# An output gate built from tanh, two halves for every output, and rows fetched two outputs in advance

## The chip, the cores and the metric

The program runs on one core of one Trainium2 chip. A core has five engines that each work through their own list of instructions in order: TensorE (PE) multiplies matrices, VectorE (DVE) and ScalarE (ACT) work element by element, GpSimd (POOL) here computes small statistics and issues some DMAs, and SyncE (SP) issues the other DMAs. An engine's list is fixed when the program is built. An instruction that waits holds up all that stand behind it on its engine.

The metric is the device time of one launch in microseconds. Before the change the median of 3 runs was 1276.79 us (1276.71 to 1282.77).

## The reference

The input x is 16 sequences of 512 tokens with 256 channels. It is normalized once (xn), and two branches work on xn. The first is a recurrent block with its own normalizations, a scan over time and a feed-forward part. The second is a mixture of 8 experts: each token goes to one expert, whose result is weighted by a router's probability. The two meet in a gate.

```python
    xn = _layernorm(x, axis=-1)
    s = _L0_attn_ref(xn, ...)              # recurrent branch
    g = _silu(_L0_ffn_ref(xn, Wg, W1, W2)) # experts, each token weighted by its router's probability
    x = x + s * g
```

In the experts' part the output row of a token is `weights * (gelu(xt @ W1[e]) @ W2[e])` for the expert e that holds the token. So the gate of a token's row y with weight w is silu(w·y), and the output is x + s·silu(w·y).

## The kernel before

The work is cut by sequence: `recurrent(b, done)` is the recurrent branch for sequence b, written as a Python generator in 9 steps. The list `steps` says in which order the 16 generators advance; three sequences are under way at a time. Beside it, `rest_of` advances other generators: the router, the weights' loads, 36 to 39 units of expert work (`expert`, 256 tokens each), and at the end `outputs`. A scheduler then orders the instructions on each engine within what the dependencies allow.

A sequence's tensors are four tiles of 128 tokens by 256 channels (1024 numbers in each of 128 partitions). In a sequence's branch come, in order:

- `normed`: statistics on DVE (L216, L218), one over the root on POOL (L209 and L210, the latter a power), the scale on ACT (L226);
- `shifted` and `mix`: transposes on PE (L234), ACT L515 and L522, DVE L523;
- the projections k, v and r on PE (L556), put out of PSUM by ACT (L628, L632, L636);
- `wkv` twice, once for each half of the channels: on DVE a scan L575, L579, L580, on ACT three Relus (L581 to L583) and an Exp (L584), then on DVE L585 to L594, with the reciprocal L593 of 3.35 us in it. Its result is vT;
- the product o with WoT (PE L599, added to x0 on DVE at L646), `normed` again (its POOL part computes nm and rs), `shifted` and `mix`;
- the products f (PE L556), each put out by ACT with Relu (L659) and squared (L660);
- twice, for half of the sequence each: a product fr (PE L599), its tanh on ACT (L669), a product kv (PE L599), then on DVE L673 and L675, which finish that half of x0, the recurrent branch's s.

PSUM buffers for fr, kv and o come from one pool of two. So kv of the second half can begin only when L673 of the first half has read kv of the first.

For b below `LATE` = 14, s is put into a scratch in memory by `keep`. The experts put their rows into another scratch, `ys_d`, by indirect DMAs from POOL (L722). When all experts have ended, a branch taken on the device (L744) separates the experts from the outputs. `outputs` then takes s (tag `w2` or `x`) and the experts' rows y (tag `w1`, two buffers) of sequences 0 to 13 back from memory, and `output` does four Silu on ACT (L755), with the router's weight as the scale of each tile, one product on DVE (L756), and one DMA from POOL (L757) that adds the product to what is in `out`. The input x had been copied to `out` earlier (L654). Sequences 14 and 15 are put out by `put` straight from x0. The outputs run while the branches of sequences 13, 14 and 15 end.

In the routing, `route` ends in a loop of four groups that makes one-hot tables on DVE (L464, L470, L473, L474) and multiplies them on PE (L479).

Of the kernel before, what the change touches and what calls it, by code (L numbers as in the profile page):

```python
# [9 lines left out]
F32 = mybir.dt.float32  # L10
I32 = mybir.dt.int32
F16 = mybir.dt.float16
AF = mybir.ActivationFunctionType
ALU = mybir.AluOpType
# [5 lines left out]
P = 128  # L20
# [6 lines left out]
def rwkv_times_moe_kernel(ctx: ExitStack, tc: tile.TileContext, a, out: bass.AP):  # L27
# [10 lines left out]
    nc = tc.nc  # L38
    x = a["x"]
    B, T, C = x.shape  # L40
# [3 lines left out]
    NJ = T // P  # L44
# [11 lines left out]
    work = ctx.enter_context(tc.tile_pool(name="work", bufs=1))  # L56
# [52 lines left out]
    place_of = const.tile([P, NJ], F32, name="place_of")  # L109
# [60 lines left out]
    ys_d = dram.tile([B * T + NR * R, C], F32, name="ys_d")  # L170
    s_d = dram.tile([B * T, C], F32, name="s_d")

    def tokens_of(t, b):

        return t[b].rearrange("(j p) c -> p j c", p=P)

    def rows_of(t, b):

        return t[b * T : (b + 1) * T].rearrange("(p j) c -> p (j c)", p=P)
# [3 lines left out]
    def flat(t):  # L183
        return t.rearrange("p j c -> p (j c)")
# [6 lines left out]
    weight_of = const.tile([P, NT], F32, name="weight_of")  # L191
# [7 lines left out]
    def load(src, b, name, tag="x", bufs=2):  # L199
        t = work.tile([P, NJ, C], F32, tag=tag, bufs=bufs, name=f"{name}{b}")  # L200
        if src is x:
            nc.sync.dma_start(t, tokens_of(x, b))
        else:
            nc.sync.dma_start(flat(t), rows_of(src, b))
        return t

    def inv_std(rs, var):

        nc.gpsimd.tensor_scalar(rs, var, EPS, None, ALU.add)  # L209
        nc.gpsimd.tensor_tensor(rs, rs, power, ALU.pow)  # L210
# [71 lines left out]
    def route():  # L282
# [117 lines left out]
        one = buf[0]  # L400
# [5 lines left out]
        ahead = work.tile([P, 1], F32, tag="prior", name="ahead")  # L406
# [52 lines left out]
        def spread(v, t0, n):  # L459
            return v[:, t0 : t0 + G, None].to_broadcast([P, G, n])  # L460

        for t0 in range(0, NT, G):
            in_lo = work.tile([P, G, P], F16, tag="kf", bufs=KF, name=f"in_lo{t0}")
            nc.vector.tensor_tensor(  # L464
                in_lo, spread(lo, t0, P), count_s[:, None, :].to_broadcast([P, G, P]), ALU.is_equal
            )

            in_hi = work.tile([P, G, 3, NS], F16, tag="ex", bufs=2, name=f"in_hi{t0}")
            one, place, seq = (in_hi[:, :, i, :] for i in range(3))
            nc.vector.tensor_tensor(  # L470
                one, spread(hi, t0, NS), count_s[:, None, :NS].to_broadcast([P, G, NS]), ALU.is_equal
            )
            nc.vector.tensor_scalar(place, one, place_of[:, t0 // B : t0 // B + 1], None, ALU.mult)  # L473
            nc.vector.tensor_tensor(  # L474
                seq, one, count_s[:, :B, None].to_broadcast([P, B, NS]), ALU.mult
            )
            yield
            for g in range(G):
                nc.tensor.matmul(  # L479
                    table, lhsT=in_lo[:, g, :], rhs=in_hi[:, g],  # L480
                    start=(t0 + g == 0), stop=(t0 + g == NT - 1),
                )
# [17 lines left out]
    def normed(src, name):  # L500

        mv = work.tile([P, NJ, 2], F32, tag="mv", bufs=3, name=f"mv_{name}")
        rs = work.tile([P, NJ], F32, tag="rs", bufs=3, name=f"rs_{name}")
        moments(mv, src, name)
        inv_std(rs, mv[:, :, 1])
        n = work.tile([P, NJ, C], F32, tag="tok", bufs=TOK, name=f"n_{name}")
        normalize(n, src, mv[:, :, 0], rs, name)
        return n
# [93 lines left out]
        if jj or n > NC:  # L602
            then_route(mm)

    def recurrent(b, done):

        xn = at_hand.pop(b) if b in at_hand else load(xn_d, b, "xc")

        g = slice(b * NJ, (b + 1) * NJ)
        r0 = work.tile([P, NJ], F32, tag="r0", bufs=2, name=f"r0_{b}")  # L610
        nc.gpsimd.tensor_tensor(r0, rs_all[:, g], rs_all[:, g], ALU.mult)
        nc.gpsimd.tensor_tensor(r0, r0, mv_all[:, g, 1], ALU.mult)
        inv_std(r0, r0)
        x0 = work.tile([P, NJ, C], F32, tag="x0", bufs=3, name=f"x0_{b}")
        for j in range(NJ):
            nc.vector.scalar_tensor_tensor(
                x0[:, j, :], xn[:, j, :], r0[:, j : j + 1], ln0w, ALU.mult, ALU.mult
            )
        nc.vector.tensor_tensor(x0, x0, ln0b[:, None, :].to_broadcast([P, NJ, C]), ALU.add)
        n1 = normed(x0, f"1_{b}")  # L620
        yield
        hp = shifted(n1, "ln1_w", "ln1_b", f"1_{b}")
        yield

        xk = mix(hp, "tmk", f"k{b}")
        kT = f4(f"kT{b}", "kT", 2)
        for o in range(NC):
            nc.scalar.copy(kT[:, o, :], project(wk, xk, o, f"k_{b}_{o}"))  # L628
        xv = mix(hp, "tmv", f"v{b}")
        vT = f4(f"vT{b}", "vT", 2)  # L630
        for o in range(NC):
            nc.scalar.copy(vT[:, o, :], project(wv, xv, o, f"v_{b}_{o}"))  # L632
        xr = mix(hp, "tmr", f"r{b}")
        erT = f4(f"erT{b}", "erT", 2)
        for o in range(NC):
            nc.scalar.activation(erT[:, o, :], project(wr, xr, o, f"r_{b}_{o}"), AF.Exp, scale=-1.0)  # L636
        yield
        for h in range(NC):
            wkv(kT, vT, erT, h, f"{b}_{h}")
            yield  # L640

        for j0 in range(0, NJ, 2):
            ps = pp_ot.tile([P, 2, C], F32, tag="ot", name=f"o_{b}_{j0}")
            for jj in range(2):
                token_major(lambda c, j: vT[:, c, j * P : (j + 1) * P], wo, NC, j0 + jj, ps, jj)
            nc.vector.tensor_tensor(x0[:, j0 : j0 + 2, :], x0[:, j0 : j0 + 2, :], ps, ALU.add)  # L646

        n2 = normed(x0, f"2_{b}")
        yield
        hp2 = shifted(n2, "ln2_w", "ln2_b", f"2_{b}")  # L650
        yield
        xk2 = mix(hp2, "cmk", f"k2{b}")
        xr2 = mix(hp2, "cmr", f"r2{b}")
        nc.sync.dma_start(rows_of(out_rows, b), rows_of(x_rows, b))  # L654
        kf = []
        for q in range(NH // 2):
            t = work.tile([P, 2, T], F32, tag="kf", bufs=KF, name=f"kf{b}_{q}")
            for o in range(2):
                nc.scalar.activation(t[:, o, :], project(wfk, xk2, q * 2 + o, f"f_{b}_{q}_{o}"), AF.Relu)  # L659
            nc.scalar.activation(t, t, AF.Square)  # L660
            kf.append(t)
        yield
        for j0 in range(0, NJ, 2):
            psr = pp_ot.tile([P, 2, C], F32, tag="ot", name=f"fr_{b}_{j0}")
            for jj in range(2):
                token_major(lambda c, j: xr2[:, c, j * P : (j + 1) * P], wfr, NC, j0 + jj, psr, jj)

            fr = work.tile([P, 2, C], F32, tag="fr", bufs=2, name=f"frs_{b}_{j0}")
            nc.scalar.activation(fr, psr, AF.Tanh, scale=0.5)  # L669
            psv = pp_ot.tile([P, 2, C], F32, tag="ot", name=f"kv_{b}_{j0}")  # L670
            for jj in range(2):
                token_major(lambda c, j: kf[c // 2][:, c % 2, j * P : (j + 1) * P], wfv, NH, j0 + jj, psv, jj)
            nc.vector.scalar_tensor_tensor(fr, fr, 1.0, psv, ALU.add, ALU.mult)  # L673
            xo = x0[:, j0 : j0 + 2, :]
            nc.vector.scalar_tensor_tensor(xo, fr, 0.5, xo, ALU.mult, ALU.add)  # L675
        done(b, x0)
        yield

    DEEP = 3
# [66 lines left out]
                pass  # L746


    def fetch(b):
        return (load(ys_d, b, "y", tag="w1"),)  # L750

    def output(b, s, y):
        for j in range(NJ):
            t = j * B + b
            nc.scalar.activation(y[:, j, :], y[:, j, :], AF.Silu, scale=weight_of[:, t : t + 1])  # L755
        nc.vector.tensor_tensor(s, s, y, ALU.mult)  # L756
        nc.gpsimd.dma_start(tokens_of(out, b), s, accum_op=ALU.add)  # L757

    def keep(b, x0):
        nc.sync.dma_start(rows_of(s_d, b), flat(x0))  # L760

    def put(b, x0):
        output(b, x0, *fetch(b))

    def outputs(bs):

        ahead = None
        for b in bs:

            now = b, load(s_d, b, "s", tag="w2" if b < 6 or b % 2 else "x"), *fetch(b)  # L770
            if ahead:
                output(*ahead)
            ahead = now
            yield
        output(*ahead)
        yield


    def each(f, items):
# [4 lines left out]

    STEPS, LATE = 9, 14
    branch = [recurrent(b, keep if b < LATE else put) for b in range(B)]
    steps = [0, 0, 0, 1, 0, 1, 0]
    for b in range(B):  # L790
        steps += [i for i in (b, b + 1, b, b, b + 1, b + 2, b, b + 1, b + 2) if i < B]
# [73 lines left out]
```

## Time and profile before

| what | us |
|---|---|
| median of 3 runs | 1276.79 |
| the profiled execution's own time | 1279.82 |
| its span, from the first to the last instruction | 1278.0 |
| mean granted clock of TensorE | 0.956 |
| PE busy in the span | 1132.0 |
| PEld (weight load) busy | 776.2 |
| DVE busy | 762.2 |
| ACT busy | 734.8 |
| POOL busy | 331.9 |

The 1.8 us between the execution's own time and its span lie outside the first and the last instruction. Times in the trace are microseconds from the span's start. The last expert's rows are written near 1098, the branch is passed near 1099, and what follows up to 1278 is called the tail here: the end of sequences 13, 14 and 15 of the recurrent branch, with all 16 outputs beside it. In rows of a group, the first number after the bar is the group's busy time, the second the mean time of one instruction in nanoseconds, and behind the second bar stands the idle time of the engine before these instructions and what ended it.

### The profile page before, as it was taken

The numbers are of one execution on the slowest core, as the hardware profiler recorded it, in microseconds if no ns is written. First come the engines' busy times: TensorE is split into PE (matmuls) and PEld (weight loads), VectorE is DVE, ScalarE is ACT, GpSimd is POOL, SyncE is SP. The second block draws the span as 40 slices with busy tenths as digits, with TensorE's granted clock in tenths as the row PEclk, the third lists the DMA queues.
The fourth block names the chain that finished last, engine by engine and source line by source line (L and its number), as shares of the span: only waits on it lengthen the run. The fifth ranks groups of instructions, "written<-read, shape, count | busy, mean of one in ns | idle before, by whom it ended". The sixth has DMA issues, their size and how long they took to land. (4 is left out here: it accounts for less than half of the span.)

```text
span 1278.0 us, 12598 instructions
## 1 busy us (share of the span) xinstructions
PE 1132.0 (89%) x4333; PEld 776.2 (61%) x4333; DVE 762.2 (60%) x1245; ACT 734.8 (57%) x1190; POOL 331.9 (26%) x427
## 2 busy tenths in 40 slices
PE   4888979579999899999999999999999989795966
PEld 2444736346668486665867667586766848463634
DVE  6887767994473727547272654727366472566651
ACT  4775774245482736638383673838356272684951
POOL 6512020051332223233241323314232210213020
PEclk9997989888999999999999999999999999898978
DMA  7761020331233122222231232223222311279391
GB/s 238 236 251 49 11 89 1 115 107 58 83 107 107 50 99 94 87 84 74 96 99 62 83 99 83 74 94 101 62 82 88 100 35 47 96 176 211 74 193 18
DMA packets 67116, 125.11 MB, mean 98 GB/s; under 512 B 5846, under 2 KB 43244, under 8 KB 66796
## 3 DMA queue, kind: packets, MB, share of 16 engines
q1 hardware_dynamic: 51692, 97.02, 22.9%
q0 software_dynamic: 15360, 27.27, 9.3%
q8 instruction: 35, 0.57, 0.2%
q14 instruction: 29, 0.24, 0.1%
HBM read 90.72 MB, written 41.94 MB: 104 GB/s over the span
## 5 line engine op out<-in xcount | busy, mean ns | idle before, releaser
L556 PE MATMUL f<-mix_k,WfkT_sb 128*128 128x512 f32 x512 | 241.2, 627 | 28.2 <-DVE mix_k L523 18.7
L599 PE MATMUL kv<-WfvT_sb,kf 128*128 128x256 f32 x1024 | 229.4, 380 | 0.0
L599 PEld LDWEIGHTS kv<-WfvT_sb,kf 128*128 128x128 f32 x1024 | 193.5, 190 | 25.7
L722 POOL DMA_INDIRECT ys_d<-ys,goes x72 | 80.0, 1111 | 494.9 <-ACT ys L720 332.9
L556 PEld LDWEIGHTS f<-mix_k,WfkT_sb 128*128 128x128 f32 x512 | 99.6, 200 | 152.7 <-issue 104.7
L673 DVE SCALAR_TENSOR_TENSOR frs<-frs,kv 128x512 f32<-128x512 f32 x32 | 21.9, 683 | 243.2 <-PE kv L599 243.1
L599 PE MATMUL y<-w,act 128*128 128x256 f32 x576 | 132.3, 380 | 2.3 <-ACT act L713 1.9
L708 PE MATMUL h<-xsT,w 128*128 128x256 f32 x576 | 130.2, 379 | 0.0
L599 PEld LDWEIGHTS y<-w,act 128*128 128x128 f32 x576 | 107.9, 190 | 23.5 <-issue 6.8
L708 PEld LDWEIGHTS h<-xsT,w 128*128 128x128 f32 x576 | 109.4, 190 | 17.0 <-issue 2.2
L691 POOL DMA_INDIRECT xs<-xn_d,holds x72 | 78.6, 1091 | 131.8 <-DVE of L489 73.1
L226 ACT ACTIVATE n<-x,nm,rs 128x256 f32<-128x256 f32 x128 | 68.5, 593 | 76.6 <-POOL nm L224 76.5
L593 DVE RECIPROCAL ex<-ex 128x512 f32<-128x512 f32 x32 | 107.2, 3351 | 0.8
L659 ACT ACTIVATE kf<-f 128x512 f32<-128x512 f32 x128 | 74.1, 593 | 47.3 <-PE f L556 46.6
L669 ACT ACTIVATE frs<-fr 128x512 f32<-128x512 f32 x32 | 19.0, 594 | 117.5 <-PE fr L599 117.4
L585 DVE TENSOR_TENSOR_SCAN ba<-ex 128x512 f32<-128x512 f32 x32 | 38.8, 1213 | 70.9 <-ACT ex L584 70.8
L556 PE MATMUL r<-mix_r,WrT_sb 128*128 128x512 f32 x128 | 65.0, 651 | 11.5 <-ACT kT L628 11.5
L556 PE MATMUL v<-mix_v,WvT_sb 128*128 128x512 f32 x128 | 63.3, 628 | 12.6 <-ACT kT L628 12.6
L599 PE MATMUL o<-WoT_sb,vT 128*128 128x256 f32 x256 | 64.3, 398 | 10.6 <-DVE frs L673 10.1
L720 ACT COPY ys<-y 128x512 f32<-128x512 f32 x27 | 15.8, 584 | 95.9 <-PE y L599 94.7
L515 ACT ACTIVATE hp<-nps,cols 128x512 f32<-128x512 f32 x64 | 48.1, 781 | 36.5 <-PE nps L234 36.5
L660 ACT ACTIVATE kf<-kf 128x1024 f32<-128x1024 f32 x64 | 67.4, 1053 | 1.1
(206 smaller groups left out, 1847.9 us busy)
## 6 DMA issues: line engine op xcount, KB each, us to landing
w<-in_W_dram SPq DMA_DIRECT2D x72, 512.0 KB, 3.7
xa<-in_x_dram SPq DMA_DIRECT2D x16, 512.0 KB, 4.6
xn_d<-xn SPq DMA_DIRECT2D x16, 512.0 KB, 7.5
out_dram<-in_x_dram SPq DMA_DIRECT2D x16, 512.0 KB, 4.3
y<-ys_d SPq DMA_DIRECT2D x16, 512.0 KB, 3.8
xc<-xn_d SPq DMA_DIRECT2D x14, 512.0 KB, 5.7
s_d<-x SPq DMA_DIRECT2D x14, 512.0 KB
s<-s_d SPq DMA_DIRECT2D x14, 512.0 KB, 3.3
```

Of the source, the lines that this page charges most:

```text
L226: nc.scalar.activation(dst[:, j, :], src[:, j, :], AF.Identity, bias=nm[:, j : j + 1], scale=rs[:, j : j + 1])
L515: nc.scalar.activation(hp[:, h, 1:], ps, AF.Identity, bias=col(bname, h), scale=col(wname, h))
L556: mm = nc.tensor.matmul(ps, lhsT=w[:, h, o * P : (o + 1) * P], rhs=src[:, h, :], start=(h == 0), stop=(h == NC - 1))
L585: nc.vector.tensor_tensor_scan(ba[:, 0, 1:], ex[:, 2, :], ex[:, 0, :], 0.0, ALU.mult, ALU.add)
L593: nc.vector.reciprocal(den, den)
L599: mm = nc.tensor.matmul(ps[:, jj, :], lhsT=lhsT_of(c, j), rhs=w[:, c, :], start=(c == 0), stop=(c == n - 1))
L659: nc.scalar.activation(t[:, o, :], project(wfk, xk2, q * 2 + o, f"f_{b}_{q}_{o}"), AF.Relu)
L660: nc.scalar.activation(t, t, AF.Square)
L673: nc.vector.scalar_tensor_tensor(fr, fr, 1.0, psv, ALU.add, ALU.mult)
L691: nc.gpsimd.indirect_dma_start(out=xs[:, j, :], out_offset=None, in_=xn_d[:, :], in_offset=rows_at(holds, 2 * i + j))
L708: nc.tensor.matmul(ps[:, ff, :], lhsT=w1[:, h, (f + ff) * P : (f + ff + 1) * P], rhs=xsT[:, h, :], start=(h == 0), stop=(h == NC - 1),)
L722: nc.gpsimd.indirect_dma_start(out=ys_d[:, :], out_offset=rows_at(goes, 2 * i + j), in_=y[:, j, :], in_offset=None)
```

## The change

There are four edits.

- In `route`, one of three one-hot tables (`place`) is made by ACT and not by DVE.
- The gate is written as silu(a) = a·(1 + tanh(a/2))/2 with a = w·y. Per sequence, DVE multiplies each of the four tiles of y by its weight (L771 in the changed file), ACT computes the tanh of each half (L773), DVE forms (tanh + 1)·a (L774), and a second DVE instruction multiplies half of that with s (L781). Each half then goes out by a DMA of its own from POOL (L782). For b below 14 both halves go out one after the other, in `finish`.
- The fetch of y runs two sequences ahead of the gate (`AHEAD_Y` = 2). Every second sequence's y is taken into two half tiles of the tag `eact` (four buffers, before only for the experts' activations), the others into a whole tile of the tag `w1`, as before. The halves of tanh use the tag `xsT` (two buffers).
- For sequences 14 and 15, `soon` fetches y and makes the gate right after the f products, and `put` puts each half out as soon as L675 of that half (now L676) is done.

```diff
@@ route @@
-            nc.vector.tensor_scalar(place, one, place_of[:, t0 // B : t0 // B + 1], None, ALU.mult)
+            nc.scalar.mul(place, one, place_of[:, t0 // B : t0 // B + 1])
@@ recurrent @@
+        soon(b)
         yield
         for j0 in range(0, NJ, 2):
...
-        done(b, x0)
+            done(b, x0, j0 // 2)
@@ outputs @@
+    fetched = [0]
     def fetch(b):
-        return (load(ys_d, b, "y", tag="w1"),)
-
-    def output(b, s, y):
-        for j in range(NJ):
-            t = j * B + b
-            nc.scalar.activation(y[:, j, :], y[:, j, :], AF.Silu, scale=weight_of[:, t : t + 1])
-        nc.vector.tensor_tensor(s, s, y, ALU.mult)
-        nc.gpsimd.dma_start(tokens_of(out, b), s, accum_op=ALU.add)
+        fetched[0] += 1
+        if fetched[0] % 2:
+            y = load(ys_d, b, "y", tag="w1")
+            return [y[:, j0 : j0 + 2, :] for j0 in range(0, NJ, 2)]
+        halves = []
+        for j0 in range(0, NJ, 2):
+            y = work.tile([P, 2, C], F32, tag="eact", bufs=4, name=f"y{b}_{j0}")
+            nc.sync.dma_start(flat(y), rows_of(ys_d, b)[:, j0 * C : (j0 + 2) * C])
+            halves.append(y)
+        return halves
+
+    def gates(b, halves):
+        for i, y in enumerate(halves):
+            for jj in range(2):
+                t = (2 * i + jj) * B + b
+                nc.vector.tensor_scalar(y[:, jj, :], y[:, jj, :], weight_of[:, t : t + 1], None, ALU.mult)
+            th = work.tile([P, 2, C], F32, tag="xsT", bufs=2, name=f"th{b}_{i}")
+            nc.scalar.activation(th, y, AF.Tanh, scale=0.5)
+            nc.vector.scalar_tensor_tensor(y, th, 1.0, y, ALU.add, ALU.mult)
+        return halves
+
+    def output(b, s, i, gate):
+        j0 = 2 * i
+        half = s[:, j0 : j0 + 2, :]
+        nc.vector.scalar_tensor_tensor(half, gate, 0.5, half, ALU.mult, ALU.mult)
+        nc.gpsimd.dma_start(tokens_of(out, b)[:, j0 : j0 + 2, :], half, accum_op=ALU.add)
...
     def outputs(bs):
-        ahead = None
-        for b in bs:
-            now = b, load(s_d, b, "s", tag="w2" if b < 6 or b % 2 else "x"), *fetch(b)
-            if ahead:
-                output(*ahead)
-            ahead = now
-            yield
-        output(*ahead)
+        ahead, behind = [], None
+        for b in [*bs, *[None] * AHEAD_Y]:
+            if b is not None:
+                ahead.append((b, fetch(b)))
+            if b is None or len(ahead) > AHEAD_Y:
+                d, halves = ahead.pop(0)
+                s = load(s_d, d, "s", tag="w2" if d < 6 or d % 2 else "x")
+                if behind:
+                    finish(*behind)
+                behind = d, s, halves
+                yield
+        finish(*behind)
         yield
...
+    def finish(b, s, halves):
+        for i, gate in enumerate(gates(b, halves)):
+            output(b, s, i, gate)
```

More of the change, by code (lines that the diff above doesn't have):

```diff
@@ L603, in token_major, with recurrent @@
             then_route(mm)
-    def recurrent(b, done):
+    def recurrent(b, done, soon):
         xn = at_hand.pop(b) if b in at_hand else load(xn_d, b, "xc")
@@ L746, in last_experts @@
                 pass
+    fetched = [0]
     def fetch(b):
-        return (load(ys_d, b, "y", tag="w1"),)
-    def output(b, s, y):
-        for j in range(NJ):
-            t = j * B + b
[L755 to L763, printed above, removed]
@@ new lines, in output, with keep, soon, put @@
+    def output(b, s, i, gate):
[3 more added lines that the diff above has]
+        nc.gpsimd.dma_start(tokens_of(out, b)[:, j0 : j0 + 2, :], half, accum_op=ALU.add)
+    def keep(b, x0, i):
+        if i == 1:
+            nc.sync.dma_start(rows_of(s_d, b), flat(x0))
+    gate_of = {}
+    def soon(b):
+        if b >= LATE:
+            gate_of[b] = gates(b, fetch(b))
+    def put(b, x0, i):
+        output(b, x0, i, gate_of[b][i])
@@ L782, in each @@
             yield
-    STEPS, LATE = 9, 14
-    branch = [recurrent(b, keep if b < LATE else put) for b in range(B)]
+    STEPS, LATE, AHEAD_Y = 9, 14, 2
+    branch = [recurrent(b, keep if b < LATE else put, soon) for b in range(B)]
     steps = [0, 0, 0, 1, 0, 1, 0]
```

## The prediction

> **What bounds the kernel now.** I read the page's slices first, then the busy time by stretches of the tail, then the waits of the tail, then the timeline at the largest of them.
>
> ```profile
> PE   4888979579999899999999999999999989795966
> DVE  6887767994473727547272654727366472566651
> 1095.00:1120.00 25.00, 15.92 (x40) 7.15 (x39) 12.07 (x27) 18.23 (x31) 5.73 (x10) 0.82 0.32 112
> 1120.00:1160.00 40.00, 31.94 (x116) 21.75 (x115) 26.48 (x23) 33.63 (x54) 6.40 (x5) 0.93 0.81 178
> 1160.00:1185.00 25.00, 17.89 (x48) 9.39 (x47) 16.15 (x28) 11.78 (x21) 8.92 (x6) 0.89 0.90 218
> 1185.00:1217.00 32.00, 31.00 (x113) 21.14 (x112) 22.76 (x19) 28.54 (x44) 2.58 (x2) 1.00 0.37 73
> ```
>
> From slice 9 to 33 PE is busy at 9 tenths: there the order of the other engines costs little. It dips in slice 7 (the routing's end, 224 to 256) and from slice 34 on (the tail). Both places are what the change touches. The columns of the four stretches are PE, PEld, DVE, ACT, POOL, granted clock, DMA share, GB/s. In the tail no engine is full: ACT has 92 of 122 us, DVE 77, PE 97. It is a chain that runs through all engines.
>
> ```profile
> POOL out_dram L757 <- DVE s L756: 99.4, 10, 29.3
> ACT n L226 <- POOL nm L224: 17.2, 3, 9.6
> DVE ba L585 <- ACT ex L584: 13.5, 2, 7.9
> PE o L599 <- DVE frs L673: 10.1, 2, 8.1
> PE r L556 <- ACT kT L628: 4.6, 1, 4.6
> L755 ACT ACT_TABLE_LOAD  x7: 1283/1283/1283, 1106.9 to 1208.5; - x7
> ```
>
> The first wait costs nothing (POOL has no other work). The fourth is the largest stall of PE in the tail, 1151.3 to 1159.4: o of sequence 14 waits for vT, and vT is late because its three Relus and its Exp on ACT ran only at 1138.7 to 1143.2, behind Silus and two table loads, though their input was ready near 1109. The fifth (1170.8 to 1175.5) comes from POOL:
>
> ```profile
> 1167.72 4.85 POOL L210 TENSOR_TENSOR rs<-rs,power 128x4 f32<-128x4 f32 x1
> 1168.24 2.35 DVE L756 TENSOR_TENSOR s<-s,y 128x1024 f32<-128x1024 f32 x2
> 1170.51 1.22 DVE L575 TENSOR_TENSOR_SCAN pp<-wcol,kT 128x512 f32<-128x512 f32 x1
> 1101.73 1.03 POOL L210 TENSOR_TENSOR rs<-rs,power 128x4 f32<-128x4 f32 x1
> ```
>
> The same power takes 1.03 us beside an idle DVE and 4.85 beside a DVE that runs instructions with two inputs back to back; it ends just after they do.
>
> **ACT in the tail.** A Silu takes 499 ns, 64 of them 31.9 us; 32 tanh of a half, at the 594 ns of L669 (a tanh of the same shape), take 19.0. Beside the seven loads above, the tail has six back to Exp's table (L584 four, L636 two). In the changed program's instruction list one load is left behind the branch: 12 go. A switch cost 1.32 us (1187.51 to 1188.83), so 15.8 us; the Trainium skill (ScalarE: Activation LUTs, What ACT_TABLE_LOAD costs) counts about 2.66 with a drain, which would be 32. The trace shows no drain; I take the row. ACT loses 12.9 + 15.8 = 28.7 us.
>
> **DVE in the tail.** It gets 64 scalings of 128x256, 32 products with tanh and 32 with s, all 128x512, for 16 products of 128x1024. Neighbours overlap by 0.09 (L523 takes 0.75 and comes every 0.66), so I count by distance: two-input 512 products 0.61 (L675), the old ones 1.14. The scaling has no row: above the 0.20 of a 128x78 scaling (L488), below the 0.48 of a two-input 128x256 (L616). I take 0.34, nearer to the one-input row, so 0.25 by distance. Sum: 64 x 0.25 + 64 x 0.61 - 16 x 1.14 = +36.8 us. DVE's 91 us from 1095 to 1250 become 128 of 155: **DVE becomes the fullest engine of the tail**, so each wait at its head moves the end.
>
> **The tail, followed in the changed order** (before -> after, both on before's clock and by before's line numbers; the order is the compiled list's).
>
> - f of 13 begins at 1117.5 -> 1116.5: erT and hp lose one load on ACT.
> - L673 of 13's first half, 1142.1 -> 1145.8. It now stands behind all of 14's second wkv. DVE from 1103.75: 20 scalings 5.0, 17 products 10.4, two first scans 2.3, eight of L579/L580/L523 5.3, two chains L585 to L593 at 8.46, one L594 0.6, together 40.5, and 1.5 of waits for ACT's mix and Exp. PE's second kv, which needs the PSUM, waits 3.9 us for it and then starts at a lower clock (after gaps of 4.4 and 4.6 us, stretches of PE took 1.7 and 1.9 us more): kv ends near 1154.9, not 1150.5.
> - But vT is there then, so o ends at 1164.0 -> 1158.6. Five us gained.
> - Normalization of 14: statistics 1166.4 -> 1161.0. POOL: DVE runs four two-input mixes (2.7) and six scalings (1.5), then stops, since tanh of sequence 6 stands on ACT behind L226, which waits for POOL. The skill (SBUF — State Buffer, Who interferes with whom) has one port pair for DVE's second read and POOL, locked by whoever starts first; by it POOL gets through at 1166.1, by the median row it would at 1164. I take 1166: L226 at 1172.9 -> 1166.3.
> - f of 14: 1184.3 -> 1178.5. DVE works 7.8 us of gate products, pp, L579, L580 off before mix_k, counted from tanh at 1170.
> - The second half of y14 is issued on SP behind the load of s10, which waits until the outputs of s6 (made at 1172.4, landing 7.7 us median) have left their buffer: it lands near 1184, and DVE stands 3 us before it. L585 of 15 at 1194.1 -> 1187.2.
> - L673 of 14's first half: 11.2 to L594, 5.2 to L580, six scalings and a product 2.1, and a wait for tanh: 1207.0 -> 1206.9. Here the gain is gone. PE's kv was ready at 1202 and stands until 1207.5.
> - vT of 15: 0.6 of L673, then its last chain with five gate instructions and L675 between, 13.1: 1218.6 -> 1220.6. o, after a gap of PE, +1; statistics +2.9; POOL behind DVE's next 3.6 us or not: f of 15 begins 3 to 6 us later, I take +4.5. From there to the end PE sets the pace in both.
>
> **The end.** After L675 came 1.23 of L756, 1.27 of issue and 3.3 us in which 0.53 MB moved (1271 to 1274.6). Now 0.69, an issue between 0.96 (L722, 128 rows) and 1.28, and half the bytes: -2.2.
>
> **The routing.** Four L473 leave DVE at 0.45 apart: -1.8. DVE is on the path there (PE waits 7.2 and 4.6 us for in_hi), ACT idles 20 us before 251.4. The same multiply on ACT lies between 0.71 (512 elements, L522) and 1.48 (1536, L584): about 1.3 each, done before the DVE instruction beside it (L474, 1.45). PE is full from there to 1095, so the gain stays; if ACT were late with the last table it would be 0.
>
> **Small ones.** Sixteen more POOL issues are 20 us on an engine that is busy 37 of the last 218. A scaling[...] meets POOL's issues: 0 to 1.28 each time; the trace of before has no such meeting. Some ten are near in the stretch from 1178 to 1220: 0 to 7, I take +1. Waits of DVE for tanh that I can't place: the list has 32 of them, +2. On ACT a tanh stands before some L659 (twice before the second f of 14); f has three PSUM buffers, so PE is held only if that tanh is over 3 us late.
>
> **Sum**: +4.5 - 2.2 - 1.8 + 1 + 2 = +3.5 against the profiled execution's 1279.8, which is 3.0 above the median of the runs shown; on the median, **1280**.
>
> **Rivals.**
>
> - *The port that DVE and POOL share decides* (1288). Place: DVE's list from mix_k of 14 to vT of 15, which is then full. Price: ten POOL issues that each hold a scaling 0.6 longer than I count (6), and POOL's power at 15's normalization shut out for all of the 3.6 us (2 more): +8 on my sum. It decides from the point at which DVE has no idle time left between 1178 and 1220; before that its holds fall into waits. For it: the 4.85 row. Against: an issue at 1138.2 ran beside an L756 of the usual 1.23.
> - *ACT's relief carries through* (1269). If y14 comes in time (-3), POOL isn't shut out (-3), PE keeps its clock (-3) and DVE's waits don't come (-2), the 5 us won at o of 14 stay: -11. For it: the chain of the tail has more ACT than DVE now. Against: the list puts both L673 behind long DVE work.
> - *The new order helps nowhere in the tail*: what is left is the routing and the end, 1279.8 - 4.0, or 1273 on the median. This needs f of 15 on time, which the DVE sum speaks against.
>
> **How the numbers follow.** 0.5% is 6.4 us, about what a measurement of this kernel can tell from no change. Forecast near 1280: 0.45. Port rival, or DVE late in another way: 0.35, nearly all of it slower. The two faster ones: 0.20 together, of which 0.12 is below -0.5%. My forecast's own range is 1274 to 1286, so it gives some to slower. Faster 0.13, same 0.48, slower 0.39. The range for 8 in 10 takes in both rivals' middles: 1267 to 1292.
>
> **What would show it.** One table load in the tail; 12 switches gone; Exp of 14's second half near 1132, not 1142. A scaling near 0.34. PE waits for L673 in both second kv, some 4 us each, and less for vT of 14. POOL's powers after the branch: long at 14 and perhaps at 15. The routing's end 1.8 us earlier. The forecast is wrong if DVE idles more than 25 us between 1103 and 1220, or if scalings take 0.5.

## The result, and the profile after

The change made the kernel a little faster: 1272.76 us median of 13 runs (1269.19 to 1275.65) against 1278.58 for 13 runs of the kernel before on the same chip, a ratio of 0.9951 with a 95% interval of 0.9937 to 0.9965. By the ratio that is -6.3 us, between -8.0 and -4.5. The forecast was +3.5 us and a time of 1280, in a range from 1267 to 1292. The time lies in that range because the range took in the rivals' middles, not because the reasoning led there: the direction is the other one.

The two profiled executions must not simply be subtracted. Their spans differ by 10.6 us, but 5.6 of it is there at 227 us, ahead of the first changed instruction (the integer slots of the routing are made at 227.06 before and at 221.43 after). So every comparison below counts from an instruction within the same trace.

The page of the changed kernel, its first lines (span; busy time, share and number of instructions of each engine):

```profile
span 1267.4 us, 12720 instructions
PE 1130.7 (89%) x4333; PEld 775.5 (61%) x4333; DVE 796.4 (63%) x1353; ACT 715.4 (56%) x1150; POOL 345.0 (27%) x443
```

DVE gained 34.2 us of work and ACT lost 19.4, as the edits say. The stretch from 1185 to 1217 of before begins 91.0 us behind the first k product of sequence 14 (1093.99). Counted in the same way from its own k product (1086.24), it is this one in the changed kernel (columns: PE, PEld, DVE, ACT, POOL, granted clock, DMA share, GB/s):

```profile
1177.25:1209.25 32.00, 25.68 (x97) 19.13 (x96) 32.00 (x42) 14.51 (x23) 8.50 (x7) 0.95 0.67 137
```

Before, PE had 31.00 of these 32 us, ACT 28.54 and DVE 22.76. Now DVE is busy for all 32.00, PE for 25.68 and ACT for 14.51: DVE has become the fullest engine of the stretch, and PE waits inside it.

PE in the tail of before, rows of its order in time (start, length, what it does, and in brackets the idle time before it with what ended it):

```profile
1093.99 3.67 PE L556 MATMUL k<-mix_k,WkT_sb 128*128 128x512 f32 x8 [0.30 <-PEq L744]
...
1159.37 4.67 PE L599 MATMUL o<-WoT_sb,vT 128*128 128x256 f32 x14 [8.06 <-DVE frs L673]
...
1184.29 14.02 PE L556 MATMUL f<-mix_k,WfkT_sb 128*128 128x512 f32 x32 [2.55 <-DVE mix_k L523]
...
1218.08 3.45 PE L599 MATMUL o<-WoT_sb,vT 128*128 128x256 f32 x14 [2.08 <-DVE frs L673]
1231.98 16.63 PE L556 MATMUL f<-mix_k,WfkT_sb 128*128 128x512 f32 x32 [2.84 <-DVE mix_k L523]
```

The same of the changed kernel:

```profile
1086.24 3.67 PE L556 MATMUL k<-mix_k,WkT_sb 128*128 128x512 f32 x8 [0.30 <-PEq L745]
...
1136.17 7.17 PE L599 MATMUL kv<-WfvT_sb,kf 128*128 128x256 f32 x32 [1.17 <-ACT frs L670]
1143.18 1.89 PE L599 MATMUL o<-WoT_sb,vT 128*128 128x256 f32 x8
1146.42 1.99 PE L599 MATMUL o<-WoT_sb,vT 128*128 128x256 f32 x8 [1.34 <-DVE frs L674]
...
1166.67 10.68 PE L556 MATMUL f<-mix_k,WfkT_sb 128*128 128x512 f32 x20 [5.24 <-DVE mix_k L523]
...
1196.83 8.86 PE L599 MATMUL kv<-WfvT_sb,kf 128*128 128x256 f32 x32 [2.90 <-DVE frs L674]
1205.52 0.59 PE L599 MATMUL o<-WoT_sb,vT 128*128 128x256 f32 x2
1208.75 3.45 PE L599 MATMUL o<-WoT_sb,vT 128*128 128x256 f32 x14 [2.63 <-DVE frs L674]
1222.92 16.72 PE L556 MATMUL f<-mix_k,WfkT_sb 128*128 128x512 f32 x32 [2.72 <-DVE mix_k L523]
```

The 8.06 us stall before o of 14 has become 1.34. What the reader is to see next is how this gain ends. Counted from the first k product of sequence 14, f of 14 starts at 90.3 before and at 80.4 after, ten us earlier; o of 15 ends at 127.5 and 126.0, and f of 15 starts at 138.0 and 136.7. Only 1.3 us is left, and further profiles of the same tail, shown below, leave nothing. Below, all such times are counted from that product, and "the tail" is the time from it to the end of the span: 184.0 before, 181.2 after.

### The profile page after: what moved, and what is told of

Read it like the earlier page. It is cut to its first block, busy times and chain, and to the rows that moved or that the text cites. A ratio compares the mean times of both kernels' runs of the same rounds, so it can differ in the third digit from the quotient of the medians.

```text
span 1267.4 us, 12720 instructions
## 1 busy us (share of the span) xinstructions
PE 1130.7 (89%) x4333; PEld 775.5 (61%) x4333; DVE 796.4 (63%) x1353; ACT 715.4 (56%) x1150; POOL 345.0 (27%) x443
## 5 line engine op out<-in xcount | busy, mean ns | idle before, releaser
L674 DVE SCALAR_TENSOR_TENSOR frs<-frs,kv 128x512 f32<-128x512 f32 x32 | 21.8, 681 | 238.9 <-PE kv L599 238.9
L585 DVE TENSOR_TENSOR_SCAN ba<-ex 128x512 f32<-128x512 f32 x32 | 38.7, 1211 | 57.2 <-ACT ex L584 57.2
```

What stands on the lines that cost most here:

```text
L585: nc.vector.tensor_tensor_scan(ba[:, 0, 1:], ex[:, 2, :], ex[:, 0, :], 0.0, ALU.mult, ALU.add)
```

## The experiments

### One line of routing, and all but that line

The first kernel is the one before with the one routing edit; the second is the changed one without it.

```diff
-            nc.vector.tensor_scalar(place, one, place_of[:, t0 // B : t0 // B + 1], None, ALU.mult)
+            nc.scalar.mul(place, one, place_of[:, t0 // B : t0 // B + 1])
```

> The kernel before with one line of the change: the four products place of the routing go from DVE to ACT, nothing else. 'The tail' is from the first k matmul of sequence 14, just behind the branch, to the end of the span: 184.0 us before, 181.2 after the whole change. Theory (the gain has two places, the routing and the tail): the routing ends 1.8 to 2.4 us sooner, the tail stays at 184.0, and the time is 1.8 to 2.4 us less, a ratio near 0.9985. Rival 1 (all of the gain is the routing's, what the tail shows is one execution's accident): the ratio of the whole change, 0.9951. Rival 2 (the routing is hidden by the PE-bound middle): ratio 1.000.

> The changed kernel with place back on DVE: the output gate, the halves and the rows fetched ahead, without the routing's line. Theory: the tail is 181.2 us as with the whole change, and the ratio lies 0.0015 above the whole change's, near 0.9966. Rival 1 (all of it is the routing): tail 181 to 184 with a ratio of 1.000. Rival 2 (the routing is hidden): ratio 0.995.

Measured: 0.9985 (0.9972 to 0.9998) for the line alone, a tail of 183.4; 0.9958 (0.9941 to 0.9976) for all else, a tail of 184.3. DVE's rows in the kernel with the line alone, from the first to the last step behind the slots:

```profile
227.26 0.20 DVE L449 TENSOR_SCALAR lo_i<-slot 128x64 int32<-128x64 int32 x1
...
253.95 0.23 DVE L490 TENSOR_TENSOR goes<-of 128x78 int32<-128x78 f32 x1
```

This takes 26.9 us (253.95 + 0.23 - 227.26); in the kernel before the same two rows stand at 227.06 and 255.56 + 0.24, which is 28.7. So the line brings 1.8 us. The stretch is 28.74 in both kernels without the line, and 26.9 in eleven of the twelve with it (27.5 in the other). Rival 1 of the first expectation is out: 0.9951 lies outside the interval. The second ratio was expected 0.0015 above that of the whole change and came 0.0007 above; its interval holds both 0.9966 and 0.9951, so it settles nothing. The tail of 184.3 was not expected: its code is that of the whole change, which gave 181.2. A single tail can't carry a difference of 1 or 2 us.

### The gate by Silu again, the rest as changed

```diff
-                nc.vector.tensor_scalar(y[:, jj, :], y[:, jj, :], weight_of[:, t : t + 1], None, ALU.mult)
-            th = work.tile([P, 2, C], F32, tag="xsT", bufs=2, name=f"th{b}_{i}")
-            nc.scalar.activation(th, y, AF.Tanh, scale=0.5)
-            nc.vector.scalar_tensor_tensor(y, th, 1.0, y, ALU.add, ALU.mult)
+                nc.scalar.activation(y[:, jj, :], y[:, jj, :], AF.Silu, scale=weight_of[:, t : t + 1])
...
-        nc.vector.scalar_tensor_tensor(half, gate, 0.5, half, ALU.mult, ALU.mult)
+        nc.vector.tensor_tensor(half, half, gate, ALU.mult)
```

> The changed kernel with the gate computed as before, four Silu on ACT with the weight as their scale, in place of the two scalings, the tanh and the product of each half; halves, fetches and routing as changed. Theory (the gain of the tail comes from ACT's relief of table loads): seven table loads and 28.7 us come back on ACT, f of 14 ends some 8 to 10 us later than with tanh, and the tail is back at 183 to 184 us or above it; only routing and end are left, ratio 0.997 to 0.998. Rival A (halves and fetches make the gain of the tail, DVE gives tanh's gain back): tail 181 us or below, since DVE is freed of 37 us, ratio 0.993 to 0.995. Rival B (ACT is worth more than the whole gain, and DVE's load gives part of it back): tail 186 us or more, ratio 0.999 to 1.001.

Measured: ratio 0.9960 (0.9947 to 0.9974), tail 182.4. f of 14 starts at 89.8, so the ten us there are the tanh's alone. At f of 15 they are gone: 138.6 with Silu, 136.7 with tanh in the whole change's first profile, and 136.7 to 139.4 in all four that have its tail. In the time, the tanh is worth no more than the intervals leave: 0.9960 against 0.9951. Of my theory, f of 14 came 9.4 us later, as expected, but the tail did not go back to 183 or more by it: 182.4 lies inside the 181.2 to 184.3 of the tails with tanh. Rival A (181 or less) and rival B (186 or more) missed as well.

### The last two sequences put out whole

```diff
     def put(b, x0, i):
-        output(b, x0, i, gate_of[b][i])
+        if i == 0:
+            return
+        for ii in range(2):
+            half = x0[:, 2 * ii : 2 * ii + 2, :]
+            nc.vector.scalar_tensor_tensor(half, gate_of[b][ii], 0.5, half, ALU.mult, ALU.mult)
+        nc.gpsimd.dma_start(tokens_of(out, b), x0, accum_op=ALU.add)
```

> The changed kernel with the last two sequences, 14 and 15, put out whole: both halves' products when the second half of the statistics is there, and one DMA of 512 KB; all else as changed. Theory (the halves shorten what follows the last matmul): from the last matmul's end to the end of the span 12.1 us again in place of 10.5, the tail 182.8 us, 1.6 us above the whole change, ratio 0.9963. Rival 1 (the first half's DMA hides nothing, both would have landed together): 10.5 us and 181.2. Rival 2 (the products in halves lie in DVE's way during sequence 15): the tail gains elsewhere what the end loses, 181.2 or less with an end of 12.1 us.

Measured: ratio 0.9977 (0.9964 to 0.9990), tail 182.9. The last row of PE in this kernel, and below it the same row of the whole change, whose spans end at 1275.0 and 1267.4:

```profile
1255.63 7.07 PE L599 MATMUL kv<-WfvT_sb,kf 128*128 128x256 f32 x32
```

```profile
1249.83 7.07 PE L599 MATMUL kv<-WfvT_sb,kf 128*128 128x256 f32 x32
```

Behind the last product 12.3 us follow (1275.0 - 1262.70) against 10.5 with halves. Three kernels that put out whole have 12.0 to 12.3, the eleven with halves 10.4 to 10.8. So the halves bring 1.8 us between these two and 1.6 between the kernel before (12.1) and the changed one; the theory had 1.6. Everything up to the last product takes as long in both (170.6 and 170.7).

### Where the ten us go: four ways to relieve DVE

From f of 14 to vT of 15 DVE is full, apart from one stop. DVE's rows and SP's, in the changed kernel:

```profile
1168.55 0.62 DVE L771 TENSOR_SCALAR y<-y,weight_of 128x256 f32<-128x256 f32 x2
1173.53 1.14 DVE L771 TENSOR_SCALAR y<-y,weight_of 128x256 f32<-128x256 f32 x4 [4.37 <-DMA y<-ys_d]
```

```profile
1162.34 0.32 SPq L762 DMA_DIRECT2D y<-ys_d  x1
1168.92 0.32 SPq L204 DMA_DIRECT2D s<-s_d  x1
1169.33 0.38 SPq L762 DMA_DIRECT2D y<-ys_d  x1
```

The second half of sequence 14's rows (its y is the twelfth fetched, so it comes in halves) is issued behind an s load that stood on SP until 1168.92 for its buffer. DVE stands 4.37 us for those rows, and what is behind them in its list, the chain to vT of 15, stands too. The chain that ended last runs through this place; three of its pieces, with their start and length:

```profile
1160.87 7.99 DMA out_dram<-s
...
1169.33 4.10 DMA y<-ys_d
...
1173.53 1.14 DVE y L771 x4
```

An earlier output had to leave its buffer first; then the s load and the rows went out, and then DVE went on. Of the four kernels the first fetches one output in advance, the second takes the scaling off DVE, the third gives the rows of 14 and 15 tiles of their own, and the fourth is the second and third together.

```diff
@@ one in advance @@
-    STEPS, LATE, AHEAD_Y = 9, 14, 2
+    STEPS, LATE, AHEAD_Y = 9, 14, 1
@@ no scaling; half_of is half of weight_of @@
-                nc.vector.tensor_scalar(y[:, jj, :], y[:, jj, :], weight_of[:, t : t + 1], None, ALU.mult)
-            nc.scalar.activation(th, y, AF.Tanh, scale=0.5)
+                nc.scalar.activation(th[:, jj, :], y[:, jj, :], AF.Tanh, scale=half_of[:, t : t + 1])
...
-        nc.vector.scalar_tensor_tensor(half, gate, 0.5, half, ALU.mult, ALU.mult)
+            nc.vector.scalar_tensor_tensor(
+                half[:, jj, :], gate[:, jj, :], half_of[:, t : t + 1], half[:, jj, :], ALU.mult, ALU.mult
+            )
@@ own tiles @@
-        fetched[0] += 1
-        if fetched[0] % 2:
+        late = b >= LATE
+        fetched[0] += not late
+        if fetched[0] % 2 and not late:
...
-            y = work.tile([P, 2, C], F32, tag="eact", bufs=4, name=f"y{b}_{j0}")
+            tag, bufs = ("xs", 2) if late else ("eact", 4)
+            y = work.tile([P, 2, C], F32, tag=tag, bufs=bufs, name=f"y{b}_{j0}")
```

> The changed kernel with the experts' rows fetched one output in advance in place of two (both kinds of buffers kept). Counted from the first k matmul of sequence 14: after the whole change f of 14 starts at 80.4, the second part of o of 15 at 122.5, and the span ends at 181.2 us. Theory (the second output in advance only keeps transfers out of DVE's way, and buffers would do with less): milestones within 1 us of these, ratio within 0.001 of the whole change's 0.995. Rival (the gain of the tail is the fetch's): DVE waits for y before several scalings, o of 15 starts 3 us later or more, tail 184 us or more, ratio 0.9975.

> The changed kernel without the 64 scalings on DVE: half the weight is the scale of the tanh on ACT (128x256, four for each output in place of two of 128x512) and the scalar of the last product on DVE (128x256, four for each output in place of two of 128x512). Theory (from f of 14 to the end of vT of 15 DVE's sum sets the time: it is full there for 32 us, so ACT's 9.9 us of lead at f of 14 is given back): 18 scalings by 0.26 to 0.34 leave DVE between the two, some 5 us, the split products bring back 1 to 1.5, o of 15's second part starts 3 to 8 us sooner than 122.5 (more than 4 only if the wait for sequence 14's own rows goes too), tail 174 to 178 us, ratio 0.989 to 0.992. Rival (PE and ACT set that stretch, a full DVE is only a filled one): o of 15 at 121.5 or later, tail 180 us or more, ratio 0.994 or more.

> The changed kernel with the rows of sequences 14 and 15 fetched into two tiles of their own (the experts' input tiles, idle by then) in place of those shared with the other outputs, so that they come early and not behind an s load that waits for its buffer. Theory (DVE's 4.37 us wait for sequence 14's second half of rows is on the chain that ends with vT of 15): the wait is gone, o of 15's second part starts 3 to 4.4 us sooner than 122.5, tail 177 to 178.5 us, ratio 0.992. Rival A (that wait only stands where DVE would wait for ACT's Exp or for kv): o of 15 stays within 1 us of 122.5, tail 181. Rival B (taking a place out of the shared buffers shifts the other outputs and fills DVE later): o sooner, but f of 15 or the end late, tail 180 or more.

> The last two edits together: no scalings on DVE, and own tiles for the rows of sequences 14 and 15. Theory (DVE sets the stretch): o of 15's second part starts 7 to 9 us sooner than 122.5, no sooner than 112.3, where PE would be the bound if f of 14 ran without waits; tail 172 to 175 us, ratio 0.988 to 0.991. Rival A (the two edits take away the same stall): no better than the better of the two alone. Rival B (PE and ACT set the stretch): tail 180 us or more.

Measured, each line from the PE rows of one trace. For the whole change four profiles count, those of the changed kernel, of the one without the routing line, of the one that puts out whole, and of the whole change run once more (in the next section). o is computed in two parts, and the column gives the start of the second, which in the last row is 8 products and not 14; in the four profiles of the whole change it lies at 122.5 to 123.5.

| kernel | ratio to before (interval) | f of 14 | o of 15 | f of 15 | last product ends | tail |
|---|---|---|---|---|---|---|
| before | 1 | 90.3 | 124.1 | 138.0 | 171.9 | 184.0 |
| whole change | 0.9951 (0.9937 to 0.9965) | 80.2 to 80.4 | 122.5 | 136.7 to 139.4 | 170.6 to 173.7 | 181.2 to 184.3 |
| one in advance | 0.9951 (0.9930 to 0.9972) | 80.6 | 120.4 | 137.0 | 171.0 | 181.4 |
| no scaling | 0.9944 (0.9924 to 0.9964) | 81.6 | 118.0 | 133.7 | 167.7 | 178.3 |
| own tiles | 0.9915 (0.9883 to 0.9947) | 79.9 | 117.1 | 132.9 | 166.0 | 176.6 |
| both | 0.9921 (0.9894 to 0.9949) | 81.8 | 117.7 | 132.2 | 165.0 | 175.8 |

The 182.9 of the kernel that puts out whole counts in the fourth tail less its longer end, 181.2. One output in advance does as well as two in the time. This run changes more than the depth, though: sequence 14's y becomes the eleventh fetched and comes as a whole tile, and DVE's wait for rows falls from 4.4 to 1.3 us. Its o of 15 starts 2.1 us sooner and then takes 5.80 us, not 3.45. The depth alone is compared in the next section. Own tiles took 5.4 us off o of 15 and 4.6 off the tail, a little more than the theory of the stall had. DVE's waits of that kernel from 1160 to 1225, with what each was for (total us, times, longest):

```profile
DVE y L776 <- ACT th L775: 5.6, 2, 3.0
DVE ba L585 <- ACT ex L584: 1.9, 1, 1.9
```

No wait for rows is left. Two new ones have come, for ACT's tanh and Exp, so DVE isn't the only engine on the chain any more. Taking the scalings away helped less in the time than expected (a ratio of 0.9944, not 0.989 to 0.992), though o of 15 came 4.5 us sooner, as forecast. It took the wait for rows away too, so its part can't be told apart, and it isn't free: ACT gets four tanh for two and DVE four last products for two. Together with own tiles it brings no more than own tiles alone. Rival A of the last expectation fits: both edits remove the same stall.

### The tanh with the stall gone, and the better kernel beside the whole change

The first of these has the Silu gate and the own tiles; the others are the whole change, own tiles with `AHEAD_Y` = 1, and own tiles once more, all on one chip.

> The gate by Silu on ACT (as in the kernel before) together with own tiles for the rows of sequences 14 and 15; routing, halves and two outputs in advance as changed. It tells what the tanh is worth once DVE doesn't stand for rows; the same with tanh had a tail of 176.6 us, Silu with the shared tiles 182.4. Theory (the tanh's lead at f of 14, 9.4 us, was kept from the end only by DVE's stall): with Silu the tail stays at 181 to 183 us, ratio 0.995 to 0.997, so that the tanh is worth 5 us or so. Rival (what own tiles bring, they bring to either gate): tail 177 to 178.5 us, ratio 0.992.

> The changed kernel itself, on the same chip as the others of this set. Theory: the tail is 181.2 us again but for clock lost by TensorE, 0 to 3 us more; ratio 0.995. Rival (181.2 was a lucky execution): tail 183 to 184.5 us, ratio 0.996 to 0.998.

> Own tiles for the rows of sequences 14 and 15, and the other outputs' rows fetched one output in advance in place of two. Theory (once 14 and 15 have their own, one in advance is enough): tail 176 to 177.5 us, ratio 0.992. Rival (with one in advance the other outputs' rows come late for DVE's scalings): o of 15's second part 2 us or more later than 117.1, tail 179 us or more.

> The changed kernel with own tiles for the rows of sequences 14 and 15 once more, beside the whole change on one chip. Theory: tail 176.6 us but for 0 to 3 us of lost clock, some 4.6 us under the whole change's, and a ratio 0.003 to 0.004 below the whole change's of this set. Rival (its first ratio, of few runs, was luck): the two ratios within 0.0015 of each other.

| kernel | ratio to before (interval) | f of 14 | f of 15 | last product ends | tail |
|---|---|---|---|---|---|
| Silu, own tiles | 0.9928 (0.9902 to 0.9955) | 90.4 | 136.4 | 169.1 | 179.6 |
| whole change | 0.9955 (0.9934 to 0.9976) | 80.3 | 138.6 | 172.3 | 182.8 |
| own tiles, one in advance | 0.9899 (0.9868 to 0.9929) | 79.9 | 132.3 | 165.7 | 176.5 |
| own tiles again | 0.9906 (0.9878 to 0.9934) | 80.0 | 132.5 | 165.3 | 175.9 |

With Silu and own tiles the tail is 179.6, between the theory and its rival. In the end of the last product, Silu with shared tiles has 171.8, tanh with shared tiles 170.6 to 173.7; with own tiles 169.1 and 165.3 to 166.0. So the tanh is worth nothing that these show while the rows come late, and, by these traces, some 3 to 4 us once they come in time. That rests on one profile with Silu, and profiles of one tail have differed by 3 us; the ratios, 0.9928 against 0.9906, point the same way, but their intervals overlap. Own tiles bring about 3 us to the Silu gate and about 6 to the tanh. ACT's waits in the kernels with Silu, first with shared tiles, then with own ones:

```profile
ACT y L771 <- DMA y<-ys_d: 22.3, 6, 8.0
```

```profile
ACT y L773 <- DMA y<-ys_d: 20.3, 5, 7.5
```

The sum hardly moves, so it isn't the number to read here; which of these waits lay on the chain wasn't followed further. The whole change came out 1.6 us slower in the tail than in its first profile, inside the theory's 0 to 3. Own tiles again are 6.9 us under it in the tail and 0.0049 in the ratio, more than the expected 4.6 and 0.003 to 0.004, so the rival that the first ratio was luck is out. The best kernel found has own tiles and one output in advance, 1267.19 us median; its interval lies just below that of the whole change in the same set. Here only the depth differs from own tiles again, and between one and two in advance the intervals overlap: the depth of the fetch brought nothing that can be measured.

## Why the prediction was wrong, point by point

**The routing** was right: four instructions of 0.45 off DVE, -1.8 forecast and measured. **The end** was right in kind: -2.2 forecast, -1.6 measured. These two together are the rival "the new order helps nowhere in the tail", which gave -4.0 and 1273 us, and which I had set aside because of the DVE sum.

**The step that failed is "f of 15 begins 3 to 6 us later, I take +4.5"**, with the allowances of +1 and +2 behind it. Counted from the k product, f of 15 stands at 138.0 before (137.3 in the kernel with the routing line alone, whose tail is the old one) and at 136.7, 136.7, 138.6 and 139.4 in the four profiles of the changed tail, on average 137.9. The term was about 0, not +4.5. The last product ends at 171.8 on average against 171.9 (171.4 with the line alone), so the allowances have nothing to show either. Going back along the forecast's own steps:

- *"PE's second kv, which needs the PSUM, waits 3.9 us for it"*: the wrong buffer for sequence 13. Its second kv starts at 1136.17, 1.17 us after PE was done with fr, and what released it was ACT's tanh of that fr. L674 of the first half runs only when kv is under way:

```profile
1138.14 0.64 DVE L674 SCALAR_TENSOR_TENSOR frs<-frs,kv 128x512 f32<-128x512 f32 x1
```

  So the second kv needn't wait until kv of the first half is read: going by what released it, it took the one of the two PSUM buffers that its own fr had left. For sequence 14 it did wait for L674, 2.90 us where the forecast had 5.5. The kv of 13 lost no clock (7.17). The statistics of 14 end at 64.8, where the forecast had 67.0 (1161.0 - 1094.0).
- *POOL "gets through at 1166.1"*: it wasn't shut out. The row that answers to the 4.85 of before, in the changed kernel:

```profile
1152.38 1.57 POOL L210 TENSOR_TENSOR rs<-rs,power 128x4 f32<-128x4 f32 x1
```

- Without these two waits f of 14 starts at 80.4 where the forecast had 84.5: it won 9.9 us, not 5.8.
- *"DVE stands 3 us"* for the second half of y14: right in mechanism, 4.37 in size, and it took 1.4 of the surplus back. L585 of 15 stands at 90.6 (forecast 93.2), vT of 15 ends at 123.0 to 124.1 (forecast 126.6; before 124.6 and, in the kernel with the routing line alone, 123.9).

So **DVE becomes the fullest engine** was right and so was "here the gain is gone"; the arrival at vT of 15 was put 2.5 to 3.6 us too late, for two waits that did not come, and the way from there to f of 15 0.6 to 2.3 us too long (15.9 forecast, 13.6 to 15.3 measured, 13.4 before). *DVE's sum* was sized well: +36.1 us from the k product to the end (96.15 to 132.23) against +36.8, and a scaling takes 0.347 us in the median against 0.34. *The tables* were right: one load behind the branch. *ACT's relief* was put too high: 24.3 us there (114.25 to 89.97), not 28.7. The working counted Silus by their length of 0.499, where they overlap as DVE's neighbours do; with seven loads of 1.28 their line had 37.41 us, so 64 Silus are 28.4 and not 31.9. *The port rival* priced ten POOL issues at 0.6 us each on a scaling; the 64 scalings have a mean of 0.374 against the median of 0.347, which is 1.7 us for whatever held them.

**What stays open.** The rows place 1.8 us in the routing and 1.6 at the end, 3.4 in all, of a measured 6.3 (4.5 to 8.0). The kernels with the routing line start the first expert's product 33.9 to 34.4 us behind the slots, those without it 36.6 and 38.3; that is a further 0.4 to 2.6 us. Some of it may reach the end: from the slots to the k product of 14 the twelve kernels with the line take 863.3 to 867.1 us, 864.9 on average, and the two without it 866.9 and 868.3. The averages differ by 2.8 us, but the ranges overlap, and it wasn't isolated. The ratios of the parts (-1.9 us for the line, -3.3 between the whole end and the halves, both with intervals of about 2 us) neither need nor exclude it.

## What to carry to other kernels

A gain on one engine is worth what is left of it at the next place where all chains meet: follow it to there, and look at who stands in between, and in what order that engine's own queue puts its waits. When work moves to an engine that becomes full, look for a stop inside its list as well as at its sum: here one transfer, issued behind another that waited for its buffer, held the tail back by 5 to 7 us, while taking all 64 new scalings away, once it was gone, brought less than a microsecond of tail and nothing in the time. And where two executions of unchanged code differ by as much as the effect, compare stretches within a trace and repeat the profile.

## What the runs showed of the hardware

**The same products behind the same gap ran at different clocks in different executions.** The second kv of 14 in two executions of the changed kernel, behind gaps of 2.90 and 3.08 us (the granted clock is the third number from the end):

```profile
1196.83:1205.60 8.77, 8.77 (x33) 7.40 (x34) 8.77 (x11) 1.25 (x3) 2.82 (x3) 0.81 0.81 217
```

```profile
1201.41:1208.50 7.09, 7.09 (x33) 6.26 (x34) 7.09 (x9) 1.26 (x3) 1.20 (x1) 1.00 0.81 230
```

At 0.81 the 32 products took 8.86 us, at 1.00 7.17. f of 15, the same 32 products in all kernels, took 15.4 to 17.1 us behind two gaps that add up to 7 to 10 us; f of 14 took 14.02 in the kernel before, at a granted clock of 1.00. Such differences make part of the 3 us between tails of the same code: 1.7 us of it is o of 15, which took 3.45 us at a clock of 1.00 in one and 5.14 at 0.67 in another, behind gaps of 2.63 and 2.73. What decides the clock wasn't tried.

**POOL's power beside DVE depends on what DVE runs.** L210 took 1.03 to 1.05 us beside an idle DVE. In the two kernels in which it met a SCALAR_TENSOR_TENSOR, two 1024-element TENSOR_TENSOR and a scan in a row on DVE it took 4.85 both times. Beside SCALAR_TENSOR_TENSOR of 512, two inputs and back to back as well, it got in after the first (1.51 to 1.57 in ten executions), once after a scan (1.91), and beside twelve scalings in a row, eight of them still to come, it took 2.08 in three executions. The Trainium skill (SBUF — State Buffer, Who interferes with whom) says that whoever issues first has the shared ports for one whole instruction. That fits the cases of 1.51 to 1.57. Which of two waiting engines comes next it leaves open, and that decided in the longer cases: I took the one row of 4.85 for the rule. Whether the kind or the length of the instructions makes the difference wasn't tried.
